# Six additions of a gather laid in two groups over two later steps (graph attention and convolution, one core)

## The chip, the cores and the metric

One core of one Trainium2 chip. The metric is the device time of one execution in microseconds. Before the change the median of three runs is 2187.2 us.

## What is computed

Two layers on N = 3327 nodes with 512 features and a dense adjacency matrix, all in fp32:

```python
h = relu(layernorm(x))
a = (h @ Wq.T + bq) @ (h @ Wk.T + bk).T / sqrt(512) + adj + adj
x = x + softmax(a) @ (h @ Wv.T + bv)
h = relu(layernorm(x))
A2 = adj + eye
d = diagonal(A2) ** -0.5
x = x + relu((d[:, None] * A2 * d[None, :]) @ (A2 @ h @ W.T))
```

The change lies in the three large products of an N x N matrix with an N x 512 one: the attention weights times h, and A2 times a block twice. The kernel calls them g = 0, 1, 2.

## The kernel before

N is padded to 26 tiles of 128 rows. A first phase (to about 630 us) makes the unnormalised attention weights and stores them and some of their sums in DRAM. The second phase, where the change lies, runs the three products g. Each is a 2 x 2 block product by Strassen's scheme with seven block products in the order `ORDER = ("p5", "p1", "p6", "p7", "p2", "p3", "p4")` (L30). So p7 is the fourth.

Each block product covers two strips of columns: a wide one (s = 0, operations of 448 or 896 elements) and a narrow one (s = 1, 384 or 768). A strip has seven steps: six pair steps (t = 0 to 5), each on two tiles of the contracted dimension, and a single step (t = None) on the thirteenth tile. A pair step is again Strassen's scheme at a smaller size:

- `Step.load` (L789) puts the left operand into one of five slots (`a_ring`, L682) by two transfers on SP's queue. A slot is free again when PE has used it.
- `Step.sums` (L793) makes three sums on VectorE (DVE), `four_sums` (L171): L173, L174 and L175, in one of three slots.
- `Step.multiply` (L801) issues seven matmuls on TensorE (PE), L813, each of which the trace shows as two. The first of them (p1; in step t = 0 it is the last) reads the left operand itself; the next ones (p6, p7, p5) need L174 and L173.

A single step has no sums: four matmuls, L805, straight from the left operand.

At the end of a strip a `Gather` brings the eight results of the small scheme from PSUM into SBUF: `first` (L837 to L845) after the step t = 5, `rest` (L850 to L861) after the single step. Then `settle` (L863) adds the gathered block to, or subtracts it from, the result blocks r11, r12, r21 and r22. For most products that is two additions or none. For p7 it is three for each of two halves k:

```python
yield nc.vector.tensor_add(r21[k], to, r12[k])        # L869
yield nc.vector.tensor_sub(r12[k], r22[k], r12[k])    # L870
yield nc.vector.tensor_sub(r22[k], r21[k], r22[k])    # L871
```

The order of every engine is written out by hand: all of this phase stands in an `in_order` block, so that each engine runs its instructions as `run(k)` (L1123) issues them. `run(k)` loads step k+3, issues the matmuls of step k, and then works off a list `waiting` of generators of DVE work. Its entries are, in this order: the sums of step k+2, in a single step the settling, and the "flow" of step k. The flow is what else is due in this step: the four differences of a right operand (L180 to L183, on DVE, `Right.make`), a job (L896, `Job.make`: one addition for a sum of the adjacency, with its store to DRAM by ACT's queue afterwards), and later the row work. In the steps around p7's settling the list is worked off whole in its own step (L1176 and L1177, `do(first_of(waiting))`). `added` counts the entries that may stay.

So behind the single step of p7, called k from here, DVE has: the rest of the gather, the sums of k+2, the six settling operations, the flow of k, the sums of k+3, and so on. The settled blocks are next used by the settling of the following product, and in g = 2 by transposes (L995, `turned`) for output rows from step k+3 of the narrow strip on (L1087).

Of the kernel before, what the change touches and what calls it, by code (L numbers as in the profile page):

```python
# [47 lines left out]
def graph_layers_kernel(  # L48
# [60 lines left out]
    def bank(k, name):  # L109
        return banks.tile([P, BW], F32, name=name, tag=f"bank{k}")  # L110
# [472 lines left out]
    def seven():  # L583
        return {r: bank(ROLE[r], r) for r in ("p6", "p7", "p5", "p2", "p3", "p4", "p1")}
# [108 lines left out]
    def deliver(before):  # L693
        while posted and posted[0][0] < before:
            posted.pop(0)[1]()

    def set_up():

        free = [view(k, j)[:, 2 * m : 2 * m + 2] for k, j in ((2, 2), (3, 0), (3, 1), (3, 2)) for m in range(2)]
        free = [f.rearrange("p a w -> p (a w)") for f in free] + [mid(k, [P, H[0]], f"ct{k}") for k in range(10)]  # L700
        for s in range(2):
            cts[s] = [[free.pop()[:, : H[s]] for d in range(DC)] for y in range(2)]
        cts["to"] = [free.pop() for k in range(2)]
# [296 lines left out]
    def turn_last(i):  # L1000
        turned_last[i] = turned(i, (0,), LAST[i - 20])
# [101 lines left out]
    for k in range(2):  # L1103
        for _ in steps[k].sums():
            pass
    banks_of, gathers = {}, {}
    waiting = []

    def flow(tasks):
        for what, args in tasks:  # L1110
            yield from what(*args) or (None,)

    def first_of(parts):
        while parts:
            for _ in parts[0]:
                yield
            parts.pop(0)

    def do(part, n=None):
        for _ in itertools.islice(part, n):  # L1120
            pass

    def run(k):  # L1123
        step, now[0] = steps[k], k
        if k + 3 < len(steps):
            steps[k + 3].load()
        if step.t == 0:
            banks_of.update(seven())
        if not cts:
            set_up()  # L1130
        if step.t is None:
            banks_of["p8"] = bank(ROLE["p1"], "p8")
        t = step.t
        for what, args in between.get(k, ()):
            if "load" in what.__name__:
                what(*args)
        if t == PAIRS - 1:
            gathers[step.r, step.s] = Gather(step.r, step.s, k == len(steps) - 2)
        gatherer = gathers.get((step.r, step.s))
        weighs = any((k, j) in inserted for j in range(7))  # L1140
        if k in sums_of and not waiting:
            do(sums_of.pop(k)())
        for j, _ in enumerate(itertools.chain((None,), step.multiply(banks_of))):
            for w, n in inserted.get((k, j), ()):
                w.product(n)
            if j == 4 and t == PAIRS - 1 and gatherer.last:
                gatherer.first(banks_of)
            for what, args in within.get(k, ()) if j == 4 else ():
                what(*args)
            if j == 2 and k in sums_of:  # L1150

                sums = sums_of.pop(k)()
                do(sums, 4)
                waiting.insert(1, sums)
            elif weighs and j > 0:
                do(first_of(waiting), 2)
        deliver(k)
        if t is None:
            do(first_of(waiting))
            if gatherer.last:  # L1160
                flags.append(nc.values_load(bad, min_val=0, max_val=1))
                for n, names in enumerate((("p2", "p3"), ("p4", "p8"))):
                    gatherer.rest(banks_of, names)
                    for i in range(20 + 3 * n, 23 + 3 * n):
                        turn_last(i)
            else:
                gatherer.rest(banks_of)
        added = 2 + (t is None)
        waiting.append(steps[k + 2].sums() if k + 2 < len(steps) else iter(()))
        if t == PAIRS - 1 and not gatherer.last:  # L1170
            do(first_of(waiting))
            gatherer.first(banks_of)
        if t is None:
            waiting.append(gatherer.settle())
        waiting.append(flow([(what, args) for what, args in between.get(k, ()) if "load" not in what.__name__]))
        if (k + 1, 0) not in inserted and (k + 1, 1) not in inserted:  # L1176
            do(first_of(waiting))  # L1177
        while len(waiting) > added:
            do(waiting.pop(0))

    with in_order(*(e.engine for e in (nc.vector, nc.tensor, nc.gpsimd, nc.scalar, nc.sync))):
        for k in range(len(steps)):
            run(k)
        deliver(len(steps))
        now[0] = len(steps)
        for n, i in enumerate(range(20, NT)):
            finish(i, (0,), LAST[n], nc.scalar if n in (3, 4) else nc.sync)
        deliver(len(steps) + 1)
# [376 lines left out]
```

## Time and profile before

| what | us |
|---|---|
| three runs | 2187.48, 2184.74, 2187.20 |
| profiled execution | 2190.65 |
| its span, first to last instruction | 2188.9 |
| PE busy, matmuls | 2168.6 |
| DVE busy | 1665.0 |
| L173, 252 operations | 257.2 |
| L174 and L175, 219 operations each at 448 or 384 columns | 129.5 each |
| L869, L870, L871 on 896 elements, one | 1.08 to 1.09 |
| L869, L870, L871 on 768 elements, one | 0.95 to 0.96 |

The page comes from one profiled execution, which took 2190.65 us, 3.45 more than the median of the runs. A row of the timeline gives the start in us, the time in us, engine, line, operation, operands with their shapes, the count and, in brackets, how long the engine was idle before it and what released it. A row of the waits gives the total in us, how often, and the longest. A row of the view by stretches gives the stretch, its length, the busy time and count of PE, PEld (weight loads), DVE, ACT and POOL, the granted PE clock as a share of full speed, the busy share of the DMA engines and GB/s. A matmul's record overlaps the next one's, so PE's busy time does not tell how fast it runs.

### The profile page before, as it was taken

The numbers are of one execution on the slowest core, as the hardware profiler recorded it, in microseconds if no ns is written. First come the engines' busy times: TensorE is split into PE (matmuls) and PEld (weight loads), VectorE is DVE, ScalarE is ACT, GpSimd is POOL, SyncE is SP. The second block draws the span as 40 slices with busy tenths as digits, with TensorE's granted clock in tenths as the row PEclk, the third lists the DMA queues.
The fourth block names the chain that finished last, engine by engine and source line by source line (L and its number), as shares of the span: only waits on it lengthen the run. The fifth ranks groups of instructions, "written<-read, shape, count | busy, mean of one in ns | idle before, by whom it ended". The sixth has DMA issues, their size and how long they took to land.

```text
span 2188.9 us, 21095 instructions
## 1 busy us (share of the span) xinstructions
PE 2168.6 (99%) x6424; PEld 1198.7 (55%) x6424; DVE 1665.0 (76%) x3250; ACT 238.8 (11%) x363; POOL 48.6 (2%) x60
## 2 busy tenths in 40 slices
PE   9999999999999999999999999999999999999998
PEld 6555555455555555555454555555666655555555
DVE  6369888888876698886878778887576567778686
ACT  5312112111110000000110000000011100000011
POOL 2000000000000000000111000000000000000000
PEclk9999999999999999999999999999999999999999
DMA  8568888888979899888797889986645468756685
GB/s 288 176 227 306 293 299 282 298 291 302 321 273 298 297 372 325 278 283 314 251 314 261 303 279 363 322 295 226 200 152 192 141 202 276 255 183 214 214 303 195
DMA packets 300374, 583.68 MB, mean 267 GB/s; under 512 B 34518, under 2 KB 168028, under 8 KB 300252
## 3 DMA queue, kind: packets, MB, share of 16 engines
q1 hardware_dynamic: 265102, 512.76, 69.5%
q10 hardware_dynamic: 35150, 69.48, 8.7%
q8 instruction: 53, 0.87, 0.2%
q14 instruction: 69, 0.57, 0.1%
HBM read 414.28 MB, written 167.85 MB: 266 GB/s over the span
## 4 chain that ended last, share of the span: by engine, by line
PE 93%; DVE 4%; DMA 2%; issue 1%; SPq 0%; ACT 0%; POOL 0%; DVEq 0%; POOLq 0%
PE p L813 52%; PE Y L454 13%; PE Z L454 7%; PE p L805 5%; PE p L905 4%; PE pw L966 3%; PE X L454 3%; PE Y L347 2%; PE Z L347 1%; DVE part L173 1%; DMA part<-sum 1%; PE mm L306 1%; PE tp L327 1%; PE pt L995 1%; PE X L347 0%
## 5 line engine op out<-in xcount | busy, mean ns | idle before, releaser
L813 PE MATMUL p<-part,b 128*128 128x448 f32 (+1 forms) x3528 | 1266.4, 514 | 5.6 <-DVE part L174 5.5
L813 PEld LDWEIGHTS p<-part,b 128*128 128x128 f32 x3528 | 669.0, 190 | 544.1 <-issue 288.7
L173 DVE TENSOR_TENSOR part<-part 128x896 f32<-128x896 f32 (+1 forms) x252 | 257.2, 1021 | 71.3 <-DMA part<-p 32.8
L454 PE MATMUL Y<-qt,hp 128*128 128x448 f32 (+1 forms) x832 | 308.4, 513 | 2.2 <-DVE g L466 2.2
L454 PEld LDWEIGHTS Y<-qt,hp 128*128 128x128 f32 x832 | 157.8, 190 | 136.3 <-issue 72.3
L454 PE MATMUL Z<-qt,hp 128*128 128x384 f32 (+1 forms) x416 | 162.5, 513 | 0.0
L175 DVE TENSOR_TENSOR part<-part,part 128x448 f32<-128x448 f32 (+1 forms) x219 | 129.5, 591 | 15.6 <-DVE part L174 0.9
L174 DVE TENSOR_TENSOR part<-part,part 128x448 f32<-128x448 f32 (+1 forms) x219 | 129.5, 591 | 7.2
L805 PE MATMUL p<-part,b 128*128 128x448 f32 (+1 forms) x336 | 124.2, 513 | 0.0
L454 PEld LDWEIGHTS Z<-qt,hp 128*128 128x128 f32 x416 | 78.8, 190 | 67.4 <-issue 37.2
L458 DVE SCALAR_TENSOR_TENSOR g<-g,Y 128x384 f32<-128x384 f32 (+1 forms) x156 | 91.6, 587 | 31.3 <-PE Y L454 27.6
L805 PEld LDWEIGHTS p<-part,b 128*128 128x128 f32 x336 | 63.7, 190 | 53.5 <-issue 31.4
L841 ACT COPY part<-p 128x384 f32<-128x384 f32 (+1 forms) x33 | 16.6, 503 | 664.7 <-PE p L813 549.3
L454 PE MATMUL X<-qt,hp 128*128 128x384 f32 (+1 forms) x208 | 81.1, 512 | 0.0
L461 ACT ACTIVATE g<-g 128x768 f32<-128x768 f32 (+1 forms) x48 | 43.1, 898 | 347.4 <-DVE g L458 276.9
L905 PE MATMUL p<-w,ct 128*128 128x512 f32 x136 | 61.8, 594 | 0.5 <-DVE part L917 0.5
L842 DVE TENSOR_TENSOR part<-p,part 128x384 f32<-128x384 f32 (+1 forms) x33 | 19.3, 586 | 54.8 <-PE p L813 54.0
L454 PEld LDWEIGHTS X<-qt,hp 128*128 128x128 f32 x208 | 39.5, 190 | 33.1 <-issue 19.3
L200 POOL TENSOR_TENSOR rstd<-ve,mhalf 128x1 f32<-128x1 f32 x52 | 42.7, 823 | 572.1 <-DVE ve L198 541.8
L966 PE MATMUL pw<-w,rows 128*128 128x256 f32 x208 | 53.6, 380 | 0.8 <-DVE rows L956 0.8
L896 DVE TENSOR_TENSOR job<-job 128x896 f32<-128x896 f32 (+1 forms) x52 | 53.0, 1019 | 0.0
L466 DVE TENSOR_TENSOR g<-g,Z 128x384 f32<-128x384 f32 (+1 forms) x52 | 30.5, 586 | 27.0 <-PE Z L454 26.7
(176 smaller groups left out, 1700.8 us busy)
## 6 DMA issues: line engine op xcount, KB each, us to landing
part<-sum SPq DMA_DIRECT2D x104, 448.0 KB, 5.1
part<-p SPq DMA_DIRECT2D x91, 448.0 KB, 5.9
part<-sum SPq DMA_DIRECT2D x104, 384.0 KB, 3.7
part<-p SPq DMA_DIRECT2D x91, 384.0 KB, 4.6
part<-in_adjT_dram SPq DMA_DIRECT2D x78, 448.0 KB, 4.7
b<-row SPq DMA_DIRECT2D x234, 128.0 KB, 4.7
part<-in_adjT_dram SPq DMA_DIRECT2D x78, 384.0 KB, 3.8
g<-in_adjT_dram SPq DMA_DIRECT2D x52, 448.0 KB, 4.4
```

The lines of the kernel that those rows point to most:

```text
L173: yield nc.vector.tensor_add(o[:, 0:2], g[:, 0:4:3], g[:, 1:2].to_broadcast([P, 2, g.shape[-1]]))
L174: yield nc.vector.tensor_add(o[:, 2], o[:, 1], g[:, 0])
L175: yield nc.vector.tensor_add(o[:, 3], o[:, 2], g[:, 2])
L347: nc.tensor.matmul(ps[:, :w], M[B[name]][:, c, o * P : (o + 1) * P], hp[k][:, A[name], c], start=start and c == 0, stop=c == 1, skip_group ...
L454: nc.tensor.matmul(ps[:, :wd], h_of(self.t, name, k), qt[B[name]][:, k], start=start and k == 0, stop=k == 1, skip_group_check=True)
L458: nc.vector.scalar_tensor_tensor(a[n], a[n], 2.0, ps[:, :wd], op0=ALU.mult, op1=ALU.add if sign > 0 else ALU.subtract)
L461: nc.scalar.activation(g[1], g[1], AF.Exp, **({"bias": pad} if self.t == HALF - 1 else {}))
L805: yield nc.tensor.matmul(ps[("p2", "p3", "p4", "p8")[k]][:, :w], b[:, z], a[:, 0, y], start=k == 3, stop=True)
L813: yield nc.tensor.matmul(ps[r][:, :w], b[:, i], m, start=self.t == 0, stop=self.t == PAIRS - 1 and r in ("p1", "p5", "p6", "p7"))
L896: nc.vector.tensor_add(self.a, self.a, self.b)
L905: nc.tensor.matmul(ps, cts[s][y][d][:, k * P : (k + 1) * P], w[d], start=d == 0, stop=d == DC - 1)
L966: nc.tensor.matmul(ps, a, W[B[name]][:, c], start=new and c == 0, stop=c == 1, skip_group_check=True)
```

## The change

The six settling operations of p7 are no longer issued in one piece in the single step k. They are cut after the third (`itertools.islice(settle, 3)`, one half of the block each) and put in a list `resting`. Each of the two next steps takes one part and sets it behind its own sums: k+1 issues the sums of k+3, then L869 to L871 of the first half; k+2 issues the sums of k+4, then those of the second half. The flow of each step stands last, as before. This happens at six places: p7 in both strips of g = 0, 1 and 2. Which instructions there are, and the order on PE, SP, ACT and POOL, stay the same; some of SP's and ACT's transfers wait on another DMA semaphore than before.

```diff
     banks_of, gathers = {}, {}
+    resting = []
     waiting = []
...
-        if t is None:
+        if t is None and gatherer.r == "p7":
+            settle = gatherer.settle()
+            resting.extend((itertools.islice(settle, 3), settle))
+            added -= 1
+        elif t is None:
             waiting.append(gatherer.settle())
+        elif resting:
+            waiting.append(resting.pop(0))
+            added += 1
         waiting.append(flow([(what, args) for what, args in between.get(k, ()) if "load" not in what.__name__]))
```

## The prediction

> **What bounds the kernel now.** I read the page's busy times first, then who TensorE (PE) waited for, then the order of VectorE (DVE) around the fourth product p7, then the granted clock there.
>
> ```profile
> PE 2168.6 (99%) x6424; PEld 1198.7 (55%) x6424; DVE 1665.0 (76%) x3250; ACT 238.8 (11%) x363; POOL 48.6 (2%) x60
> ...
> PE 93%; DVE 4%; DMA 2%; issue 1%; SPq 0%; ACT 0%; POOL 0%; DVEq 0%; POOLq 0%
> ```
>
> PE is busy for 2168.6 of 2188.9 us, and 93% of the chain that ended last is PE. So little of the span is open to a reordering: only what PE loses while idle or slowed. The list of PE's waits says where.
>
> ```profile
> PE p L813 <- DVE part L174: 5.5, 5, 1.9
> PE Y L454 <- DVE g L466: 2.2, 1, 2.2
> ```
>
> Five waits, 5.5 us together, are for L174, the second of a step's three sums. PE's own timeline gives their places: before the matmuls that start at 877.93 (1.93 us idle), 1339.54 (0.58), 1422.31 (1.06), 1454.71 (0.86) and 1955.68 (1.06). All but 1339.54 stand two to three steps behind a settling (L869 starts at 868.96, 1414.20, 1445.40, 1947.57). DVE's timeline at the first:
>
> ```profile
> 866.37 0.62 DVE L861 TENSOR_TENSOR part<-part,p 128x448 f32<-128x448 f32 x1
> 866.90 0.95 DVE L173 TENSOR_TENSOR part<-part 128x768 f32<-128x768 f32 x1
> 867.89 0.56 DVE L174 TENSOR_TENSOR part<-part,part 128x384 f32<-128x384 f32 x1
> 868.48 0.56 DVE L175 TENSOR_TENSOR part<-part,part 128x384 f32<-128x384 f32 x1
> 868.96 1.08 DVE L869 TENSOR_TENSOR ct<-part,ct 128x896 f32<-128x896 f32 x1
> ...
> 874.46 1.09 DVE L871 TENSOR_TENSOR ct<-ct,ct 128x896 f32<-128x896 f32 x1
> 875.47 0.95 DVE L896 TENSOR_TENSOR job<-job 128x768 f32<-128x768 f32 x1
> 876.33 0.95 DVE L173 TENSOR_TENSOR part<-part 128x768 f32<-128x768 f32 x1
> 877.32 0.56 DVE L174 TENSOR_TENSOR part<-part,part 128x384 f32<-128x384 f32 x1
> ```
>
> With k the single step of the strip, the sums at 866.90 are those of step k+2. Six settling additions and one job follow without idle time, and only at 876.33 the sums of k+3. PE has done k+1, k+2 and the first matmul of k+3 by 876.00 and stands until L174 ends.
>
> **After this stall PE also runs slow.** The view by stretches, where a row's last three figures are the granted clock, the DMA share and GB/s:
>
> ```profile
> 876.00:878.00 2.00, 0.07 (x2) 0.07 (x1) 1.93 (x4) 0.00 (x0) 0.00 (x0) 1.00 0.71 260
> 878.00:882.00 4.00, 4.00 (x8) 2.21 (x9) 3.83 (x6) 0.00 (x0) 0.00 (x0) 0.57 0.41 110
> 882.00:892.00 10.00, 10.00 (x33) 5.89 (x32) 6.72 (x13) 0.00 (x0) 0.00 (x0) 1.00 0.94 316
> ```
>
> Eight matmuls in 4 us against 33 in 10 us: PE is "busy" but at clock 0.57. That costs (1 - 0.57) x 4 = 1.72 us which no list of waits shows. The three other stalls are followed by clock 1.00 (1410 to 1460 and 1940 to 1990).
>
> [...]
>
> **The change, part by part.** No instruction is added or removed; PE, SP, ACT and POOL keep their order. At the three wide and three narrow settlings, DVE's order becomes: sums of k+2, flow of k, sums of k+3, three settling operations, flow of k+1, sums of k+4, three settling operations, flow of k+2. Pitches from DVE's timeline, start to start: narrow sums 2.06 (866.90 to 868.96), wide sums 2.32 to 2.4; three settling operations on 896 elements 3.25 (868.96 to 872.21), on 768 2.86 (1445.40 to 1448.26); a job 0.86; four differences (L180 to L183) 0.93. PE takes 4.53 us for a narrow pair step, 5.26 for a wide one.
>
> First place (876.00). Job at 868.96: its second load is issued at 864.20, and that transfer's landing there takes 4.4 us, so it is in by 868.6. Sums of k+3 from 869.8, their L174 done at 871.4; PE asks at 876.00, so 4.6 us of cover. Then half the settling to 875.1, sums of k+4 with L174 done at 876.7 against PE's need at 880.5 (3.8 us), the other half to 880.4, sums of k+5 done at 882.0 against 885.1 (3.1). The step data are in: the second half of k+3's left side is issued at 858.09, of k+4's at 863.35 (landed 866.74). The stall goes, and with it the slow clock.
>
> Third (1421.25) and fifth (1954.62), the wide strips of the other graphs: the same sums. L174 of k+3 is done at 1415.7 and 1949.1 against needs of 1421.2 and 1954.6; k+4 at about 1422 and 1954.4 against 1425.6 and 1959.1. Both stalls go.
>
> Fourth (1453.85), narrow strip. Four differences and the job now stand before the sums of k+3. The job's loads at 1441.40 and 1441.82 share the queue with four weight loads; the first landed at 1446.83, so I put the job at 1447.4. Sums of k+3: L174 done at 1450.0 against 1453.85; k+4 1456.1 against 1459.1; k+5 1462.2 against 1464.4. The thinnest cover is 2.2 us. The stall goes.
>
> Second (911.15) and sixth (1987.21): only the weight load waits 0.7 us. PE's idle time shows nothing, but matmul starts there are some 0.26 us apart over their usual 0.376; I count 0.26 each. In the sixth the settled block r22 is read by transposes (L995) at the end of step k+3, at 1991.83. Its last addition, before at 1984.6, now ends near 1991.1, 0.45 us before PE comes. If this cover is gone, PE waits by what is lacking, tenths of a microsecond.
>
> Sum: idle 1.93 + 1.06 + 0.86 + 1.06 = 4.91. A matmul's record lasts 0.16 to 0.22 longer than its start-to-start share, so each of the four stalls costs about 0.17 above its idle time: 0.7. Slow clock 1.72. Two hidden waits 0.5. Together 7.8 us; I take 7.6 for the thin sixth place. Unknown: the slow clock (0 to 1.72 in the median) and whether sums later in DVE's queue are late (0 to 3). Nothing else is late next: DVE's position after the second half is the one it has before (880.44 for k+5 against 880.51), and PE's next need is 2 us or more behind it everywhere. 1339.54 (0.58) hangs on a store and reload of a job and stays.
>
> The profiled execution took 2190.65 us for a span of 2188.9, and the median of the three runs is 2187.2, 3.5 below it. I take the loss from the median: 2187.2 - 7.6 = 2179.6.
>
> **Rivals.**
> - The slow clock is the profiled execution's alone. For it: [...]the profiled execution is slower than all three runs. Against: 1.93 us of idle is in the program's order, in every run. Then 7.6 - 1.72 = 5.9: 2181.3.
> - The wait moves instead of going: a half settling before the sums of k+4 and k+5 makes those late, with half the loss left, 5.9 / 2 = 3.0: 2184.2. Against it stand covers of 2.2 to 3.8 us; for it, that the fourth place hangs on a job whose landing I estimate.
> - Slower: SP's loads behind the settling wait on other transfers' semaphores (in the first place the load of k+8 now waits for one that it did not wait for before; a job load was held for it earlier). SP serves in order, so a late store would hold all later loads. The data of k+8 land at 889.27 and PE needs them at 899.7: 10.4 us of cover, 6.6 with PE 3.8 earlier. It decides from lateness over 6.6 + 7.6 / 3 = 9.1 us at each of three places. With 11 us late, a stall of 4.4 and a slow clock of 1.7 at each: 3 x 6.1 - 7.6 = 10.7 more, 2197.9. Against: such transfers land in 3.4 to 6.5 us here, and the job's store is now earlier, not later.
> - The change does nothing because DVE's order is the same: 2187.2. The two programs' DVE orders differ at all six places, so this is nearly excluded.
>
> **How the numbers follow.** All stalls go 0.64; clock not in the median 0.15; half comes back 0.14; slower 0.04; nothing 0.03. A measurement of this kernel can tell about 0.2%, 4.4 us, from no change, so faster means below 2182.8. From the likeliest nearly all counts as faster (0.62), from the second most (0.12), from the third a quarter (0.04): 0.78. Same: 0.18. Slower: 0.04. The three runs spread over 2.7 us, so the likeliest alone is 2177 to 2182. The range: below, the lowest run less the sum, 2184.74 - 7.8 = 2176.9; above, to 2184.4, just over the half-loss case.
>
> **What would show it.** In the profile after: PE's wait for L174 falls from 5.5 in five to about 0.6 in one (the job's reload); no stretch with clock near 0.5 behind the first settling of p7; the sums of k+3 start within 1 us of the end of those of k+2 plus a job; DVE's busy time stays 1665; the span falls by 7 to 8 us. Wrong if PE waits for L174 of k+4 or k+5, if L995 waits for L871, if DVE waits for the job before k+3, or if SP's loads come later against PE than before.

## The result and the profile after

The changed kernel takes 2178.43 us (median of 12 runs, 2176.49 to 2182.44), the kernel before 2186.55 us (12 runs, 2183.37 to 2188.96) beside it. The ratio is 0.9965 with a 95% interval of 0.9957 to 0.9973: 7.65 us less (5.9 to 9.4), worked out from this ratio; the two medians lie 8.1 apart. Forecast were 7.6 us less and 2179.6 us.

The page's busy times and the shares of the chain, kernel after:

```profile
PE 2163.2 (99%) x6424; PEld 1197.1 (55%) x6424; DVE 1664.5 (76%) x3250; ACT 238.4 (11%) x363; POOL 49.0 (2%) x60
...
PE 95%; DVE 3%; DMA 1%; issue 1%; ACT 0%; POOL 0%; DVEq 0%; POOLq 0%
```

The same instructions, and DVE's time within 0.5 us. PE is idle for 7.1 us less (20.3 before, 13.2 after) and busy for 5.4 us less; a stretch at half clock counts as busy (in the kernel before, 4.00 of 4.00 us at clock 0.57 behind the first stall). The waits of PE, kernel after (total, times, longest):

```profile
PE Y L454 <- DVE g L466: 0.3, 1, 0.3
PE p L813 <- DVE part L174: 0.2, 1, 0.2
PE p L813 <- DVE part L858: 0.2, 1, 0.2
```

The wait for L174 has gone from 5.5 us in five places to 0.2 in one. DVE's timeline at the first place, kernel after:

```profile
862.45 0.62 DVE L861 TENSOR_TENSOR part<-part,p 128x448 f32<-128x448 f32 x1
862.98 0.95 DVE L173 TENSOR_TENSOR part<-part 128x768 f32<-128x768 f32 x1
...
865.04 0.95 DVE L896 TENSOR_TENSOR job<-job 128x768 f32<-128x768 f32 x1
865.90 0.95 DVE L173 TENSOR_TENSOR part<-part 128x768 f32<-128x768 f32 x1
866.89 0.56 DVE L174 TENSOR_TENSOR part<-part,part 128x384 f32<-128x384 f32 x1
867.48 0.56 DVE L175 TENSOR_TENSOR part<-part,part 128x384 f32<-128x384 f32 x1
867.96 1.08 DVE L869 TENSOR_TENSOR ct<-part,ct 128x896 f32<-128x896 f32 x1
...
871.21 0.95 DVE L173 TENSOR_TENSOR part<-part 128x768 f32<-128x768 f32 x1
...
873.34 1.08 DVE L869 TENSOR_TENSOR ct<-part,ct 128x896 f32<-128x896 f32 x1
...
876.59 0.95 DVE L173 TENSOR_TENSOR part<-part 128x768 f32<-128x768 f32 x1
```

The sums of k+3 start at 865.90, 3.45 us behind the start of L861; before they came 9.96 us behind it (866.37 and 876.33). PE's own timeline there, first in the kernel before:

```profile
866.16 9.84 PE L813 MATMUL p<-part,b 128*128 128x384 f32 x30
877.93 19.38 PE L813 MATMUL p<-part,b 128*128 128x384 f32 x54 [1.93 <-DVE part L174]
```

and in the kernel after:

```profile
859.24 3.17 PE L805 MATMUL p<-part,b 128*128 128x448 f32 x8
862.24 27.25 PE L813 MATMUL p<-part,b 128*128 128x384 f32 x84
889.33 2.74 PE L805 MATMUL p<-part,b 128*128 128x384 f32 x8
```

All 84 matmuls of the six pair steps run in one piece: no bracket with an idle time. The two stretches at the same times as those at the stall before:

```profile
876.00:878.00 2.00, 2.00 (x7) 1.14 (x6) 1.97 (x3) 0.00 (x0) 0.00 (x0) 1.00 0.83 254
878.00:882.00 4.00, 4.00 (x14) 2.36 (x13) 3.75 (x7) 0.00 (x0) 0.00 (x0) 1.00 0.89 246
```

Clock 1.00, and 14 matmuls in 4 us where there were 8.

**The two spans differ by more than the runs.** They are 2188.9 and 2176.4 us, 12.5 apart. To tell what belongs to the change I take the starts of L858, the first addition of the gather's second part, in each of the six p7 strips from DVE's timeline, and the first L995 behind the sixth from PE's:

| stretch | before | after | less |
|---|---|---|---|
| start to first place | 864.11 | 860.19 | 3.92 |
| first to second | 34.16 | 30.27 | 3.89 |
| second to third | 511.08 | 510.42 | 0.66 |
| third to fourth | 31.32 | 29.99 | 1.33 |
| fourth to fifth | 502.05 | 500.93 | 1.12 |
| fifth to sixth | 31.32 | 29.99 | 1.33 |
| sixth to first L995 | 17.78 | 17.52 | 0.26 |
| first L995 to the end | 197.03 | 197.12 | -0.09 |

The first row lies ahead of everything that was changed. There PE waits at about 632 us for DVE (L466, 2.2 us in the kernel before and 0.3 in the kernel after), and in the kernel before a half clock follows this wait (0.50 from 635.73 to 639.14). With the same instructions up to there this wait was 0.2 to 2.5 us in the profiles of this study. The row from the second to the third place also holds something else, the wait at 1339.54: it is 0.58 us before and 0.16 after.

To leave that out I take PE's timeline from the start of one single step (L805) to the next, across each place. In order of the six places the change saves 3.89, 0.26, 1.33, 1.13, 1.33 and 0.26 us, 8.2 together; 1.70 of the first is the half clock, by the profiles without one that follow below. So 8.2 us of the 12.5 belong to the six places, and 6.5 without the half clock.

### The profile page after: what moved, and what is told of

It reads as the page before. It is cut to its first block, busy times and chain, and to the rows that moved or that the text cites. A ratio compares the mean times of both kernels' runs of the same rounds, so it can differ in the third digit from the quotient of the medians.

```text
span 2176.4 us, 21093 instructions
## 1 busy us (share of the span) xinstructions
PE 2163.2 (99%) x6424; PEld 1197.1 (55%) x6424; DVE 1664.5 (76%) x3250; ACT 238.4 (11%) x363; POOL 49.0 (2%) x60
## 4 chain that ended last, share of the span: by engine, by line
PE 95%; DVE 3%; DMA 1%; issue 1%; ACT 0%; POOL 0%; DVEq 0%; POOLq 0%
PE p L813 54%; PE Y L454 13%; PE Z L454 7%; PE p L805 5%; PE p L905 4%; PE pw L966 3%; PE X L454 3%; PE Y L347 2%; PE Z L347 1%; PE mm L306 1%; DMA part<-sum 1%; PE tp L327 1%; DVE part L173 1%; PE pt L995 1%; PE X L347 0%
## 5 line engine op out<-in xcount | busy, mean ns | idle before, releaser
L174 DVE TENSOR_TENSOR part<-part,part 128x448 f32<-128x448 f32 (+1 forms) x219 | 129.4, 591 | 7.2
L805 PE MATMUL p<-part,b 128*128 128x448 f32 (+1 forms) x336 | 124.2, 513 | 0.0
L805 PEld LDWEIGHTS p<-part,b 128*128 128x128 f32 x336 | 63.7, 190 | 53.5 <-issue 31.2
L466 DVE TENSOR_TENSOR g<-g,Z 128x384 f32<-128x384 f32 (+1 forms) x52 | 30.5, 586 | 26.8 <-PE Z L454 26.4
```

The costliest lines, as they stand in the source:

```text
L174: yield nc.vector.tensor_add(o[:, 2], o[:, 1], g[:, 0])
L805: yield nc.tensor.matmul(ps[("p2", "p3", "p4", "p8")[k]][:, :w], b[:, z], a[:, 0, y], start=k == 3, stop=True)
```

## The experiments

Each is measured beside runs of the kernel before on the same chip. Differences in us are the ratio times the median of before there (2185.60 in the first four, 2185.92 in the next four, 2186.44 in the last).

**One strip at a time.**

```diff
-        if t is None and gatherer.r == "p7":
+        if t is None and gatherer.r == "p7" and step.s == 0:
```

> The settling is cut and moved in the wide strip only (three places); the three narrow ones stay as before the change. Theory (each stall of TensorE behind a settling is paid by itself, and the first also pays a stretch at half clock): 1.93 + 1.06 + 1.06 us idle, about 0.5 for refilling after three stalls, 1.72 of slow clock, together 6.3 us less than before; waits of TensorE for L174 left: 0.86 (fourth place) and what hangs on the job's reload. Rival (the slow clock is not paid in the runs that are timed): 4.6 us less.

Measured: 2180.76 us, ratio 0.9974 (0.9967 to 0.9981), 5.7 us less (4.2 to 7.2). One wait for L174 is left, 0.9 us, in the fourth place as expected. The interval holds both 6.3 and 4.6, so it says nothing on the half clock.

```diff
-        if t is None and gatherer.r == "p7":
+        if t is None and gatherer.r == "p7" and step.s == 1:
```

> The settling is cut and moved in the narrow strip only; the three wide ones stay in one piece. Theory: 0.86 us idle and 0.17 of refill in the fourth place, 0.26 each in the second and sixth, together 1.5 us less than before; waits for L174 of 1.93, 1.06 and 1.06 stay in the profile. With the run of the wide strip alone it should make up the 7.65 us of the whole change. Rival (what was gained is one thing that either part brings, a shift of all later transfers for example): this alone brings 3 us or more. The profile also shows once more whether 1.93 us of idle time brings the half clock.

Measured: 2183.93 us, ratio 0.9992 (0.9985 to 0.9998), 1.7 us less (0.4 to 3.3). The waits of PE, kernel with only the narrow strips changed:

```profile
PE p L813 <- DVE part L174: 4.0, 3, 1.9
```

The three wide stalls stay, 1.93, 1.06 and 1.06. The two parts make 5.7 + 1.7 = 7.4 of the whole's 7.65, so the gain adds up by place: the stalls are paid one by one.

**The order without the cut.**

```diff
-            resting.extend((itertools.islice(settle, 3), settle))
+            resting.append(settle)
```

> All six settling operations stand behind the sums of k+3, uncut. Theory (what counts is that the sums of k+3 come first; behind them there is room): from the timeline of the kernel before, L174 of k+4 would be done at 880.0 in the first place against a need at 880.5, in the third at 1425.2 against 1425.6, in the fourth at about 1459.0 against 1459.1. So 7.0 to 7.6 us less than before, at most tenths of waiting for L174 of k+4. Rival (the cut is what matters, DVE being late for k+4 with six operations ahead): waits of 1 us and more before k+4 in the three wide strips, 3 to 4 us less than before.

Measured: 2178.43 us, ratio 0.9966 (0.9953 to 0.9979), 7.4 us less (4.6 to 10.3), and no wait for L174 in the list of PE's waits. What counts is that the sums of k+3 stand ahead of the settling. That it is cut in two is not needed; it leaves more room before k+4. In the first place L174 of k+4 ends at 876.16 here, 0.4 us before the first matmul that needs it starts (876.58); in the changed kernel it ends at 872.76, 3.7 us before (876.43).

**The flow ahead, the settling where it was.**

```diff
-        if t is None:
-            waiting.append(gatherer.settle())
         waiting.append(flow([(what, args) for what, args in between.get(k, ()) if "load" not in what.__name__]))
+        if t is None:
+            waiting.insert(len(waiting) - (gatherer.r != "p7"), gatherer.settle())
```

(This is against the kernel before; for other products than p7 the order is the old one.)

> The settling stays in one piece in the single step and ahead of the sums of k+3; only the flow of that step (job and differences) is put ahead of it. Theory: TensorE waits for the sums of k+3 as before, five waits of 5.5 us together for L174, time equal to before within 1 us. Rival (the gain comes from the job and its store leaving six operations earlier, so that SP is not held for a DMA semaphore): 1 to 3 us less than before.

Measured: 2185.62 us, ratio 0.9999 (0.9991 to 1.0008), between 2.0 us less and 1.7 more: no change that can be seen. The time alone leaves the lower part of the rival's 1 to 3 us open; the profile does not. The stalls behind the settling, 1.93, 1.06, 0.85 and 1.06, are all there, and from the third place to the fourth it takes 31.32 us as before. An earlier job and store bring nothing; the rival falls.

This profile brought what the prediction could not see. The stretch of the first stall and what follows it, first in the kernel with only the narrow strips changed:

```profile
872.20:874.20 2.00, 0.07 (x2) 0.06 (x1) 1.93 (x4) 0.00 (x0) 0.00 (x0) 1.00 0.79 255
874.20:878.20 4.00, 4.00 (x9) 2.18 (x10) 3.83 (x6) 0.00 (x0) 0.00 (x0) 0.66 0.41 113
```

and then in the kernel with the flow ahead:

```profile
873.30:875.30 2.00, 0.08 (x1) 0.00 (x0) 1.93 (x4) 0.00 (x0) 0.00 (x0) 1.00 0.80 228
875.30:879.30 4.00, 4.00 (x13) 2.41 (x14) 3.83 (x6) 0.00 (x0) 0.00 (x0) 1.00 0.59 198
```

The same 1.93 us without a matmul, once with clock 0.66 in the 4 us behind it and 9 matmuls, once with 1.00 and 13. From the first place to the second these profiles take 34.16 and 32.47 us, so the half clock costs 1.69 us when it comes.

**Longer stalls.** To the kernel before, further additions of the gathered block to itself are added once it has been used, one per settling and then two:

```diff
                     yield nc.vector.tensor_add(r21[k], to, r12[k])
+                    if k == 0:
+                        yield nc.vector.tensor_add(to, to, to)
```

> The kernel before, with one more addition on VectorE in every settling of p7 (on the gathered block after its last use, so nothing that is kept changes): 1.12 us more in the three wide, 0.97 in the three narrow. TensorE's stalls become about 3.05, 2.18, 1.83 and 2.18 us in the first, third, fourth and fifth place, 1.1 in the second and sixth. Sum of the additions 6.3 us. Theory (a stall of 1.9 us or more brings a half clock of 1.7 us in some executions and not in others[...]): 6.3 and about half of four times 1.7 less the half of one that is paid already, together 8 to 10 us more than before; the profile shows a half clock behind some of the four. Rival (1.93 us always brings it): 11.5 more, four of four. Rival (timed runs never pay): 6.3 more.

Measured for one addition more: 2194.09 us, ratio 1.004 (1.0027 to 1.0054), 8.7 us more (5.9 to 11.8). Its profile has stalls of 2.94, 2.06, 1.73 and 2.07 in the four places and a half clock behind the first alone. The rival's four of four is refuted.

> As the one with longer stalls, with two more additions in every settling (one in each half): stalls of about 4.2, 3.3, 2.8 and 3.3 us, and 2.1 in the second and sixth place. The additions make 12.6 us. Theory (the longer the stall, the surer the half clock): nearly all of the four and half of the other two pay 1.7 us, 18 to 21 us more than before, and at least four half clocks in the profile. Rival (timed runs do not pay): 12.6 more.

(The second has the addition without the `if`.) Measured: 2200.52 us, ratio 1.0075 (1.0061 to 1.0089), 16.4 us more (13.3 to 19.5). Less than expected, and the profile has two half clocks and not four. Two stalls of 3.07 us in this one profile, each with the 4 us behind it:

```profile
1421.00:1424.50 3.50, 0.43 (x3) 0.05 (x1) 3.40 (x5) 0.00 (x0) 0.00 (x0) 1.00 0.60 205
1424.50:1428.50 4.00, 4.00 (x13) 2.41 (x14) 3.86 (x6) 0.00 (x0) 0.00 (x0) 1.00 0.35 109
1958.00:1961.60 3.60, 0.53 (x3) 0.05 (x1) 3.50 (x5) 0.00 (x0) 0.00 (x0) 1.00 0.42 145
1961.60:1965.60 4.00, 4.00 (x8) 2.20 (x9) 3.83 (x6) 0.00 (x0) 0.00 (x0) 0.59 0.01 4
```

One is followed by full speed and one by 0.59. So even 3.07 us do not make it sure: my "the longer, the surer", which no run had shown, left out where the stall falls (last section). My 12.6 us for the additions was too much as well. Across the six places each one delays PE by 1.00 us in a wide strip and 0.87 in a narrow one, 11.2 in all. 16.4 - 11.2 leaves 5.2, three half clocks of 1.7 within the interval; this one profile has two.

**How much cover is there.** The changed kernel with further additions in each half:

```diff
                     yield nc.vector.tensor_add(r21[k], to, r12[k])
+                    for _ in range(2):
+                        yield nc.vector.tensor_add(to, to, to)
...
-            resting.extend((itertools.islice(settle, 3), settle))
+            resting.extend((itertools.islice(settle, 5), settle))
```

> The changed kernel with one more addition in each half of the settling (on the gathered block after its last use; nothing that is kept changes). Theory (cover of 2.2 us and more before the sums of k+5, 0.45 us before the transposes): each half takes 1.12 us more in wide strips and 0.97 in narrow ones, 2.24 and 1.94 by the sums of k+5, which the cover takes without a wait; but the transposes of the sixth place wait some 1.5 us for L871's last addition. So 7.65 - 1.5 = 6.1 us less than before. Rival (the cover is thinner than worked out, the wait has only moved): waits for L174 of k+5 in three places and more, 3 us less than before or none.

(There it is one addition, and the cut is behind the fourth.) Measured: 2179.97 us, ratio 0.9972 (0.996 to 0.9983), 6.1 us less (3.7 to 8.7). Its waits of PE:

```profile
PE pt L996 <- DVE part L872: 1.1, 1, 1.1
```

No wait for L174 at all; the one new wait is where the cover was worked out to be thinnest, the transposes of the sixth place (L995 and L871 have moved by a line). Expected were 1.5 us.

> The changed kernel with two more additions in each half of the settling (nothing that is kept changes). Theory: the cover of k+4 holds (3.8 less 2.2), that of k+5 does not: waits for its L174 of about 1.4, 1.7, 1.7 and 0.9 us in the first, third, fourth and fifth place, and 3.4 before the transposes in the sixth, together 9.1 us: 1.5 us more than before, up to 5 with half clocks. Rival (the cover was larger than worked out): 3 us less than before or better, few waits.

Measured: 2190.47 us, ratio 1.0024 (1.0014 to 1.0035), 5.2 us more (3.1 to 7.7). Its waits:

```profile
PE p L813 <- DVE part L174: 5.9, 6, 1.6
PE pt L997 <- DVE part L873: 3.1, 1, 3.1
```

In the first, third, fourth and fifth place PE stands 1.33, 1.34, 0.71 and 0.47 us (expected 1.4, 1.7, 1.7 and 0.9), and the transposes 3.1 (3.4). A stall of 1.58 in the second place was not expected; my expectation did not name that place, though the cover of about 2 us in the prediction would have given it. The whole was expected at 1.5 us more, up to 5 with half clocks. The refilling, about 0.27 us at each of six pauses, was left out there, and the profile has one half clock, behind the transposes' wait. So the cover before k+5 ends between the further work of the last run and of this one: 2.0 and 4.3 us in a wide strip, 1.7 and 3.7 in a narrow one. That is about where it was worked out.

**The first stall alone, for the half clock.**

```diff
-        if t is None and gatherer.r == "p7":
+        if t is None and gatherer.r == "p7" and (step.g, step.s) != (0, 0):
```

> The change at five of the six places; in the first place (wide strip, g = 0) the settling stays in one piece, so that the stall of 1.93 us is there and alone. Theory (the half clock behind it comes in some executions only): from the gather of the first place to that of the second 32.5 us without a half clock and 34.2 with it, 30.3 being the time without the stall; time 3.7 to 5.4 us less than before, by the share of executions that pay 1.7 us, between the two ends. Rival (always paid): 3.8 less, 34.2 in every profile. Rival (timed runs never pay): 5.4 less.

> The same kernel once more, for a second profile: 1.93 us of idle time in the first place, and either 32.5 us (no half clock) or 34.2 (half clock) to the second place's gather.

> The same kernel, third profile: again 32.5 or 34.2 us. With the three profiles that have the stall of 1.93 us so far (two with a half clock, one without), theory expects both kinds among the new ones; always-paid expects 34.2 each time.

> The same kernel, fourth profile: again 32.5 or 34.2 us, for the count.

Measured in the first: 2181.99 us, ratio 0.9979 (0.997 to 0.9989), 4.6 us less (2.4 to 6.6), between both ends and not deciding. The four profiles do better: 1.93 us idle in each, 32.47 us from the first to the second place in all four, no half clock (in the first of them clock 1.00 and 13 matmuls in the 4 us behind the stall). With the three earlier profiles the half clock followed 1.93 us of idle time in two of seven.

For the timed runs there is the mean granted clock on record for each of them. One half clock lowers it by 0.0008 (1.7 of 2180 us). In the first four experiments, on one chip, it averages 0.9971 over the 79 runs that have the first stall, the kernel before among them, and 0.9970 over the 21 that do not. Worked out from the spread of the runs, that lies between -0.33 and 0.23 half clocks a run (95% interval), so at most about one run in four pays it. In the runs with two additions more per settling it averages 0.9952 over five runs, against 0.9974 in the kernel before beside it: 2.9 half clocks a run more (1.9 to 3.9). So timed runs do pay, though seldom for the first stall alone.

## Why the prediction was right, point by point

- **Which stalls go.** Right in all four places and in the two hidden ones: no idle time of 0.1 us or more is left at any of them, and the sixth gives 0.26 as counted. The cause is the order of the sums of k+3 and the settling, as the uncut version (7.4 less) and the flow alone (nothing) show.
- **Where the DVE work lands.** In the first place the sums of k+3, k+4 and k+5 were put at 869.8, 875.1 and 880.4. Less the 3.92 us by which this profile is early, that is 865.9, 871.2 and 876.5; they start at 865.90, 871.21 and 876.59.
- **The fourth place.** Too cautious: I had the sums of k+3 5.7 us behind the start of L861, and they come 4.6 behind it (1432.80 and 1437.40), since the job did not have to wait for its data, which I had put in late. Nothing hung on it.
- **The thinnest cover.** 0.45 us before the transposes; the profile after has 0.43 (L871 ends at 1978.88, L995 starts at 1979.31).
- **"Slow clock 1.72."** Right in size when it comes (1.69), wrong as a term of the sum: it follows a stall of 1.93 us in two of seven profiles and, by the clocks on record, in at most about a quarter of the timed runs. So most of it was not in the median from which it was taken off. The range from 0 to 1.72 was named, the upper end taken; that some executions do not pay was the author's estimate, since the one profile at hand had the half clock.
- **Idle time and refill.** Under-sized. A wide stall of 1.06 us gave 1.33, so refilling costs 0.27 and not 0.17. With 2.20 for the first stall without its half clock (32.47 - 30.27), the six places give 6.5 where the prediction had 6.1.
- **The sum.** 6.5, and 0 to 0.5 for the half clock, make 6.5 to 7.0; the runs say 7.65 (5.9 to 9.4). The interval holds these, the prediction's 7.6 and the 8.2 of the two profiles. That 7.6 was met so closely is in part luck: too much half clock (1.72 for 0 to 0.5) and too little refilling (0.7 for 1.1) offset each other in part.
- **1339.54 stays.** Wrong, harmlessly: 0.58 us before, 0.16 after, none with only the wide strips changed, 0.72 with longer stalls. It hangs on a store and reload of a job: 6.46 and 4.87 us on the chain before, 5.79 and 5.00 after.
- **The span falls by 7 to 8 us.** 12.5 in these two profiles, of which 3.92 lie ahead of the change and 0.4 in the reload at 1339.54; 8.2 are left for the six places.
- **The rivals.** The wait did not move: with one addition more in each half there is still no wait for L174. That SP can be held by a store, with the loads behind it, is in the trace before: behind 876.20 it issues nothing, its next load, L891, waits 3.7 us for a job's store and is issued at 879.91, and L892 and L726 follow at 880.28 and 882.50. But no wait for SP's loads appears in the list of PE's waits in the kernel after, so the semaphores on its queue did nothing that could be seen. That the slow clock is the profiled execution's alone holds for at least about three runs in four at the first stall; as a rule it is wrong, since timed runs pay after longer stalls. That every run pays it is refuted.

## What to carry to other kernels

Where PE is busy for 99%, look in the list of its waits for an operation that DVE reaches late, and then at what stands ahead of it in DVE's queue and has no reader soon. Here moving that behind the needed sums took the waits for L174 from 5.5 us to 0.2, with DVE busy for 1664.5 us where it was 1665.0. Work out the cover at the new place from pitches start to start; one as thin as the 0.43 us before the transposes should be named: with one addition more in each half, PE waited 1.1 us there. And compare two profiles stretch by stretch: a third of the difference in span here had nothing to do with the change.

## What was not expected of the hardware

A pause of PE may or may not halve its clock for 3.4 us, and its length alone does not decide. Counted behind pauses after 600 us, up to PE's last matmul, in all the profiles here: none in three of 1.73 and 1.74 us, two in seven of 1.93, none in two of 2.06 and 2.07, one each at 2.21, 2.50 and 2.94, none at 2.60, two in three of 3.07 and 3.08, one at 3.94. The shorter pauses there, up to 1.58 us, never brought it. The half clock lasted 3.4 us (0.50 over 3.41 us at 635.73 and 878.08 in the kernel before and at 1962.30 with two additions more) and cost 1.69.

What goes with it in these traces is where the pause falls. Within one profile the changes of the granted clock lie on a grid of windows of 3.413 us: in the kernel before, half clocks begin at 635.73 and 878.08, 71 windows apart, and each ends one window later, at 639.14 and 881.49. The grid does not lie alike in all executions: in the kernel after, where the clock is 0.50 for the two windows from 24.03 to 30.85, it lies 0.72 us earlier from the start of the span than in the kernel before. Here are whole windows of that grid (the first three figures are the stretch, its length and PE's busy time). First the stall of 1.93 us in the kernel before:

```profile
874.67:878.08 3.41, 1.48 (x6) 0.60 (x5) 3.34 (x5) 0.00 (x0) 0.00 (x0) 1.00 0.85 305
878.08:881.49 3.41, 3.41 (x6) 1.90 (x7) 3.24 (x5) 0.00 (x0) 0.00 (x0) 0.50 0.32 76
```

The same stall in the kernel with the flow ahead:

```profile
871.46:874.87 3.41, 1.92 (x6) 0.77 (x5) 3.31 (x5) 0.00 (x0) 0.00 (x0) 1.00 0.88 312
874.87:878.29 3.42, 2.99 (x9) 1.82 (x10) 3.25 (x6) 0.00 (x0) 0.00 (x0) 1.00 0.72 244
```

And the two stalls of 3.07 us in the kernel with two additions more:

```profile
1419.58:1422.99 3.41, 1.80 (x6) 0.76 (x4) 3.34 (x5) 0.00 (x0) 0.00 (x0) 1.00 0.95 338
1422.99:1426.41 3.42, 1.96 (x6) 1.25 (x7) 3.35 (x5) 0.00 (x0) 0.00 (x0) 1.00 0.07 23
1426.41:1429.82 3.41, 3.41 (x12) 2.00 (x11) 2.86 (x5) 0.00 (x0) 0.00 (x0) 1.00 0.68 218
1958.89:1962.30 3.41, 0.75 (x2) 0.49 (x3) 3.31 (x6) 0.00 (x0) 0.00 (x0) 1.00 0.25 75
1962.30:1965.71 3.41, 3.41 (x7) 1.87 (x6) 3.20 (x5) 0.00 (x0) 0.00 (x0) 0.50 0.02 5
```

In the kernel before all 1.93 us lie in one window, and the next one runs at 0.50; with the flow ahead they are split into 1.49 and 0.43, and the clock stays at 1.00. Of the two stalls of 3.07 the one split into 1.61 and 1.46 costs nothing further, the one with 2.66 in one window does. In the same stretch of the 14 profiles, all six windows with more than 2.1 us idle were followed by a half clock, and of three with 1.93 us two were; in the third the pause ends 0.02 us before the window does. No window with 1.72 us idle or less was. If all positions are equally likely, a pause of 1.93 us falls whole into one window with a chance of (3.41 - 1.93) / 3.41 = 0.43, an estimate from these two measured lengths; it did in three of the seven profiles. This was read from the traces afterwards: no run placed a pause in the window on purpose, and no window with between 1.72 and 1.93 us idle was measured.
